# Where q and k are turned: TensorE's transposes replaced by VectorE's 32x32 squares, ScalarE's copies and 96x96 products in a two-layer channel-attention kernel

## The chip, the cores and the metric

The kernel runs on one core of one Trainium2 chip. The metric is the device time of one execution in microseconds (us). Every time below is from executions of this kernel on the chip; durations of single instructions come from one profiled execution.

A core has five engines, each with its own queue of instructions that it works off in order. TensorE (PE in the profile) multiplies matrices into PSUM; each of its multiplications has a weight load ahead of it, which the profile lists apart as PEld. VectorE (DVE), ScalarE (ACT) and GpSimd (POOL) work on SBUF and, the first two, on PSUM. SyncE (SP) issues transfers here. An engine waits for another on semaphores.

## The reference

The input x is an image of 384 channels, 192x192, in fp32. Two layers each add something to x. The first is attention over channels; the second, which the change doesn't touch, a depthwise 7x7 convolution.

```python
# layer 0
qkv = einsum('bchw,oc->bohw', groupnorm(x), w_qkv) + b_qkv         # 384 -> 1152 channels
qkv = qkv.reshape(b, 3*c, 96, 2, 96, 2).max(axis=(3, 5))           # 2x2 max pool
qkv = depthwise_conv3x3(qkv, w_dw) + b_dw                          # 9 taps per channel
q, k, v = split(qkv, 3)                                            # each 8 heads of 48 channels, 9216 places
attn = (q / |q|) @ (k / |k|).T * temperature                       # 48x48 per head, over the 9216 places
out = sum of four top-k softmaxes of attn, each @ v * a_i
x = x + w_proj @ upsample2x(gelu(out)) + b_proj
# layer 1
x = x + depthwise_conv7x7(groupnorm(x), w_sym)
```

The product of q and k sums over the places of the image. TensorE sums over partitions, and the convolutions leave channels on the partitions, so q and k have to be turned: places to the partitions, channels along the free dimension.

## The kernel before

The work runs in stages, one after the other, and the profile's span shows them in this order.

1. **Statistics** (to about 160 us): x is read once for the group norm.
2. **q and k** (about 160 to 1389 us): 24 blocks `b` of 8 image rows (4 pooled rows of 96: 384 places, `PB`). q and k together have 768 channels, 6 tiles `ct` of 128. For each tile, `pooled` (line 639) makes 3 groups `g` of 128x512 in PSUM, each summed over 3 input tiles, and VectorE's `tensor_reduce` (line 647) takes the 2x2 maximum into `ring[ct]`. TensorE runs each fp32 product as two instructions: 54 products, 108 instructions a block. The groups use a pool of 4 PSUM buffers (`pq`), so TensorE can be at most four groups ahead of VectorE's maxima. One tile and one block behind, `depthwise` does the nine taps of block `b-1`: tap 0 is a `tensor_scalar` (line 680), taps 1 to 8 are `scalar_tensor_tensor` (line 682), all on VectorE.
   When six tiles of a block are through, `products` is called (lines 686 to 717): ScalarE squares each tile for the norms (line 691); for each of 3 runs of 128 places and each of two sides, TensorE transposes three 128x128 pieces into a PSUM tile (line 700, 18 instructions a block), ScalarE copies it to SBUF (line 706, 6 copies a block), and 3 products of 128 channels of q with 144 to 192 channels of k are added to `grams` (line 709, 18 instructions a block).
3. **The hand-over** (about 1355 to 1395 us): no further blocks come, VectorE finishes the taps of the last one, TensorE begins the v products on `xv_begun`, and the last products follow.
4. **v** (about 1390 to 2190 us): 16 steps. `convolve` (line 537) makes v; VectorE pools it (line 543) and does its taps (line 905); `attend` (line 961) multiplies v by the attention, in tiles of 128 output channels; `project` (line 985) multiplies by `w_proj`. `attention` itself (lines 772 to 862) is a long chain on VectorE that is worked off between the first v products. It scales `grams` into `scaled`, moves each head's 48x48 part into `att` by DMA, ranks it, and writes `attnT`. Output tile `ct` of 128 channels meets only those input tiles `dt` whose heads overlap it (`near`): 7 pairs of tiles, as 384 channels in heads of 48 don't fall on the bounds of 128.
5. **The 7x7 convolution** (about 2190 us to the end).

The order of instructions on an engine is not always that of the text. A scheduler in the framework reorders them, except where `keep` (`tc.keep_in_program_order`) holds them or `issue_after` sets a lower bound. In the stage for q and k, `keep` isn't used before the change, and the scheduler places the transposes and products of one block among the first groups of the next.

A tile pool with `bufs=n` gives out n buffers in turn; a tile that reuses a buffer waits until all that read the old one are done. Before: `qkp` (the results of the taps) has 9, `trp` (turned sides, squares) 2.

Of the kernel before, what the change touches and what calls it, by code (L numbers as in the profile page):

```python
# [31 lines left out]
NX = 3  # L32
GN_EPS = 1e-5


SPAN = []
for _mt in range(KT):
    _lo = (_mt * P) // HC * HC
    _hi = ((_mt + 1) * P - 1) // HC * HC + HC
    SPAN.append((_lo, _hi))  # L40

PIECES = []
for _mt in range(KT):
# [35 lines left out]
def conv_preact_d2(  # L79
# [146 lines left out]

    ssq = const.tile([P, 2 * KT, NB], F32, name="ssq")
    attnT = const.tile([P, KT, C], F32, name="attnT")


    bctx = ExitStack()
# [26 lines left out]

    psx = ExitStack()
    pgram = psx.enter_context(tc.tile_pool(name="pgram", bufs=1, space=PSUM))  # L260
    gram = []
    for mt, (lo, hi) in enumerate(SPAN):
        o = sum(h - l for l, h in SPAN[:mt])
        gram.append((o, o + hi - lo))
    grams = pgram.tile([P, gram[-1][1]], F32, name="grams")
    gram = [grams[:, lo:hi] for lo, hi in gram]
    ptr = psx.enter_context(tc.tile_pool(name="ptr", bufs=3, space=PSUM))
    qx = ExitStack()
    pq = qx.enter_context(tc.tile_pool(name="pq", bufs=4, space=PSUM))
# [216 lines left out]
        w = wq[:, TWO, i * C : (i + 1) * C]  # L486
        nc.scalar.mul(w, w, rstd0[:, TWO : TWO + 1])
    with tc.issue_after(loaded):
        nc.sync.dma_start(wp, wprojT.rearrange("(t p) o -> p t o", p=P))

# [57 lines left out]

    with ExitStack() as bx:
        padp = bx.enter_context(tc.tile_pool(name="padp", bufs=1))
        qkp = bx.enter_context(tc.tile_pool(name="qkp", bufs=9))
        trp = bx.enter_context(tc.tile_pool(name="trp", bufs=2))

        gwp = bx.enter_context(tc.tile_pool(name="gwp", bufs=1))

# [66 lines left out]
        for ct in range(2 * KT):  # L624
            ring.append(padp.tile([P, 3 * PR + 2, PS + 2], F32, name=f"ring{ct}"))

        def pooled(b, ct, xb):
            rows = xb.rearrange("p t (r c) -> p t r c", c=HW)
            t = ring[ct]
            r0 = 1 + b % 3 * PR  # L630
            for g in range(3):
                begun, there = sums_qk.pop((b, ct, g), (None, False))
                ps = begun
                if not there:
                    ps = pq.tile([P, 512], F32, name=f"pq{b}_{ct}_{g}", tag="pq")
                    if begun is not None:
                        nc.scalar.copy(ps, begun)
                for kt in range(KT) if begun is None else (TWO,):
                    nc.tensor.matmul(  # L639
                        ps,  # L640
                        wq[:, kt, ct * P : (ct + 1) * P],
                        rows[:, kt, :, g * 64 : (g + 1) * 64],
                        start=(kt == 0),
                        stop=(kt == KT - 1),
                        skip_group_check=begun is not None,
                    )
                nc.vector.tensor_reduce(  # L647
                    t[:, r0 : r0 + PR, 1 + g * 32 : 1 + (g + 1) * 32],
                    ps.rearrange("p (h a w b) -> p h w a b", h=PR, a=2, b=2),
                    AX.XY,  # L650
                    ALU.max,
                )
# [22 lines left out]
        def taps(dst, ct, win):  # L675
            for tap in range(9):
                src = win(tap // 3, tap % 3)
                w = wd[:, ct, tap : tap + 1]
                if tap == 0:
                    nc.vector.tensor_scalar(dst, src, w, bdb[:, ct : ct + 1], ALU.mult, ALU.add)  # L680
                else:
                    nc.vector.scalar_tensor_tensor(dst, src, w, dst, ALU.mult, ALU.add)  # L682

# [1 line left out]
            r0 = b % 3 * PR  # L685
            taps(dst, ct, lambda i, j: ring[ct][:, r0 + i : r0 + i + PR, j : j + PS])

        def products(b, qk):
            for i in range(2 * KT):
                junk = trp.tile([P, PB], F32, name=f"junk{b}_{i}", tag="junk")  # L690
                nc.scalar.activation(  # L691
                    junk, qk[i].rearrange("p h w -> p (h w)"), AF.Square,
                    accum_out=ssq[:, i, b : b + 1],
                )
            for j in range(PB // P):
                sides = []
                for s in range(2):
                    ps = ptr.tile([P, C], F32, name=f"tr{b}_{j}_{s}", tag="tr")
                    for i in range(KT):
                        nc.tensor.transpose(  # L700
                            ps[:, i * P : (i + 1) * P],
                            qk[s * KT + i].rearrange("p h w -> p (h w)")[:, j * P : (j + 1) * P],
                            ident,
                        )
                    sb = trp.tile([P, C], F32, name=f"qkT{b}_{j}_{s}", tag=f"qkT{s}")
                    nc.scalar.copy(sb, ps)
                    sides.append(sb)
                for mt, (lo, hi) in enumerate(SPAN):
                    last = nc.tensor.matmul(
                        gram[mt],  # L710
                        sides[0][:, mt * P : (mt + 1) * P],
                        sides[1][:, lo:hi],
                        start=False,
                        stop=(b == NB - 1 and j == PB // P - 1),
                        skip_group_check=True,
                    ).ins
            return last


        nc.tensor.matmul(  # L720
            grams, z[:, RUN : RUN + P], z[:, RUN : RUN + grams.shape[1]], start=True, stop=False,
            skip_group_check=True,
        )
        for b in range(NB + 1):
            xb = None
            if b < NB:
                xb = held.pop(b) if b in held else load_x(b, "xq")
            else:

                qx.close()  # L730
                pv = psx.enter_context(tc.tile_pool(name="pv", bufs=2, space=PSUM))
                xb = xpool.tile([P, 2 * UT, KT, RB * HW], F32, name="xv_begun", tag="xb")
                for kt in range(KT):
                    nc.sync.dma_start(xb[:, :, kt], image_rows(kt, order[0], 0, 2 * UT))
            qk = []
            for ct in range(2 * KT + 1):
                if b < NB and ct < 2 * KT:
                    if b == 0 and ct < 2:

                        if ct == 0:  # L740
                            pooled(b, 0, xb)
                            pooled(b, 1, xb)
                            biases()
                    else:
                        pooled(b, ct, xb)
                    bordered(b, ct)
                if b > 0 and ct > 0:
                    dst = qkp.tile([P, PR, PS], F32, name=f"qk{b}_{ct}", tag="qk")
                    qk.append(dst)
                    depthwise(b - 1, ct - 1, dst)  # L750
                    if ct == 2 * KT:
                        multiplied = products(b - 1, qk)
                    if b == NB:
                        with tc.issue_after(multiplied):
                            for n in ((), (), (0, 1), (), (2, 3), (4,), (5,))[ct]:
                                t0 = n // KT * UT
                                convolve(0, t0, n % KT, xb[:, t0 : t0 + UT], lambda ins: ins)
            if b == 2:
                for tiles in vrows:
                    row_borders(tiles)  # L760
            if b < len(pieces):
                with tc.issue_after(stats0):
                    weights(*pieces[b])

    xctx.close()

    near = {}

    def attention(ap):

# [13 lines left out]
        along_free(rkb, rn[:, KT : 2 * KT], ptr, "rk", "tr")  # L784
        yield

        scaled = ap.tile([P, KT, C // 2], F32, name="scaled")
        for mt, (lo, hi) in enumerate(SPAN):
            nc.vector.scalar_tensor_tensor(
                scaled[:, mt, 0 : hi - lo], gram[mt], rn[:, mt : mt + 1], rkb[:, lo:hi],  # L790
                ALU.mult, ALU.mult,
            )
        att = ap.tile([P, KT, HC], F32, name="att")
        for i, (mt, r0, r1, h) in enumerate(PIECES):
            eng = (nc.gpsimd, nc.scalar)[i % 2]
            o = h * HC - SPAN[mt][0]
            eng.dma_start(att[r0:r1, mt, :], scaled[r0:r1, mt, o : o + HC])
        yield


# [50 lines left out]
            eng.dma_start(diag[r0:r1, mt, h * HC : (h + 1) * HC], mix[r0:r1, mt, :])  # L851
        yield
        for dt in range(KT):
            cts = [ct for ct in range(KT) if SPAN[ct][0] < (dt + 1) * P and SPAN[ct][1] > dt * P]
            near[dt] = cts
            ps = ptr.tile([P, C], F32, name=f"aT{dt}", tag="tr")
            for ct in cts:
                nc.tensor.transpose(
                    ps[:, ct * P : (ct + 1) * P], diag[:, ct, dt * P : (dt + 1) * P], ident
                )  # L860
            lo, hi = cts[0] * P, (cts[-1] + 1) * P
            nc.vector.tensor_copy(attnT[:, dt, lo:hi], ps[:, lo:hi])

# [85 lines left out]
    def attend(i, pin=lambda ins: ins):  # L951
# [2 lines left out]
        gl = gp.tile([P, KT, PBC], F32, name=f"gl{b}", tag="gl")  # L954
        for h in range(2):
            for ct in range(KT):
                dts = [dt for dt in range(KT) if ct in near[dt]]
                ps = ptr.tile([P, C], F32, name=f"po{b}_{ct}_{h}", tag="tr")
                for dt in dts:
                    keep(  # L960
# [563 lines left out]
```

## Time and profile before

| | |
|---|---|
| median of 5 runs | 2798.33 us (2795.73 to 2803.1) |
| the profiled execution | 2799.82 us, span 2798.1 us, granted TensorE clock 0.994 |
| PE busy | 2646.0 us (95%), 8717 instructions |
| DVE busy | 2355.8 us (84%) |
| ACT busy | 873.9 us (31%) |
| POOL busy | 751.0 us (27%) |

Busy is the time in which at least one instruction of the engine was under way. Instructions of one engine overlap at their ends, so the mean duration of one (in ns) is longer than the distance from its start to the next one's; for matmuls by much, as their ends are modelled. In this text, the distance of starts is called the pitch, and work is priced by pitches where the trace shows a row of them. A group's line gives: line of the code, engine, operation, written tile <- read tiles, shapes, count | busy us, mean ns | idle time before it.

### The profile page before, as it was taken

To read this page: it belongs to the slowest core of one execution; us is meant where nothing else is said; L and a number is where in the kernel's file an instruction comes from. 1 tells how busy PE (TensorE), PEld (TensorE's weight loads), DVE (VectorE), ACT (ScalarE), POOL (GpSimd) and SP (SyncE) were. 2 spreads that over 40 slices of the span, in tenths; PEclk is the share of its full clock that TensorE was granted. 3 is DMA by queue.
4 is the path that set the end of the run, shared out by engine and by line. 5 is a ranking of instruction groups with operands and counts; after the bars stand their busy time and mean duration, and the time that the engine had idled before them with its cause. 6 is when DMAs were issued, how large, how long until landed. Compare 5 with 4: busy or idle time off the path is not lost. (4 is left out here: it accounts for less than half of the span.)

```text
span 2798.1 us, 25638 instructions
## 1 busy us (share of the span) xinstructions
PE 2646.0 (95%) x8717; PEld 1586.2 (57%) x8717; DVE 2355.8 (84%) x3383; ACT 873.9 (31%) x1638; POOL 751.0 (27%) x884
## 2 busy tenths in 40 slices
PE   0399999999999999999999999999999899999998
PEld 0144444444445444444556666666666677777776
DVE  7989887887877878878798988889889778888887
ACT  0141111111111111111202232222323577777776
POOL 1024343200000000000102231010101567878876
PEclk9999999999999999999999999999999999999999
DMA  9976656401001001010234998575664899999998
GB/s 380 399 251 208 235 201 220 167 34 68 34 34 68 34 34 68 34 56 13 71 134 170 336 384 312 171 251 194 210 236 153 336 328 357 367 374 373 373 373 262
DMA packets 234002, 580.98 MB, mean 208 GB/s; under 512 B 16608, under 2 KB 165712, under 8 KB 217104
## 3 DMA queue, kind: packets, MB, share of 16 engines
q1 hardware_dynamic: 173376, 283.44, 28.7%
q0 software_dynamic: 37376, 148.85, 15.1%
q10 hardware_dynamic: 23120, 147.07, 14.0%
q8 instruction: 69, 1.13, 0.2%
q14 instruction: 61, 0.50, 0.0%
HBM read 370.93 MB, written 208.21 MB: 207 GB/s over the span
## 5 line engine op out<-in xcount | busy, mean ns | idle before, releaser
L639 PE MATMUL pq<-xq,wq 128*128 128x512 f32 x2268 | 990.7, 592 | 0.0
L639 PEld LDWEIGHTS pq<-xq,wq 128*128 128x128 f32 x2268 | 423.0, 190 | 492.2 <-issue 448.2
L682 DVE SCALAR_TENSOR_TENSOR qk<-ring,wd,qk 128x384 f32<-128x384 f32 x1152 | 675.3, 614 | 20.9 <-ACT ring L669 7.1
L537 PE MATMUL pv<-xv,wq 128*128 128x384 f32 x1656 | 539.2, 486 | 1.4 <-DVE rows L543 1.4
L647 DVE TENSOR_REDUCE ring<-pq 128x128 f32<-128x512 f32 x428 | 294.2, 689 | 192.9 <-PE pq L639 191.2
L1428 PE MATMUL pc<-main,w 128*128 128x288 f32 x1536 | 438.2, 408 | 7.0 <-POOL aux L1356 3.0
L537 PEld LDWEIGHTS pv<-xv,wq 128*128 128x128 f32 x1656 | 314.3, 190 | 217.2 <-DVE rows L543 3.0
L1448 DVE TENSOR_SCALAR apart<-pc,rb 32x576 f32<-32x576 f32 x384 | 312.2, 813 | 80.9 <-PE pc L1428 59.3
L1428 PEld LDWEIGHTS pc<-main,w 128*128 128x128 f32 x1536 | 291.2, 190 | 92.4 <-POOL aux L1356 3.2
L1446 ACT ACTIVATE apart<-pc,rb 32x576 f32<-32x576 f32 x384 | 281.4, 733 | 137.4 <-PE pc L1428 132.6
L905 DVE SCALAR_TENSOR_TENSOR vb<-rows,wd,vb 128x576 f32<-128x576 f32 x384 | 313.2, 817 | 11.2
L1428 PE MATMUL pc<-aux,h 128*128 128x288 f32 x768 | 248.9, 406 | 0.3 <-issue 0.3
L691 ACT ACTIVATE junk<-qk 128x384 f32<-128x384 f32 x144 | 75.4, 524 | 543.5 <-DVE qk L682 543.5
L773 POOL TENSOR_TENSOR rn<-rn,halfpos 128x6 f32<-128x6 f32 x1 | 1.4, 1362 | 850.6 <-DVE rn L772 850.6
L1387 POOL COPY res<-apart 128x1152 f32<-128x1152 f32 (+1 forms) x96 | 224.3, 2363 | 14.0 <-ACT apart L1446 10.2
L1022 DVE TENSOR_TENSOR sx<-xr,y 128x576 f32<-128x576 f32 x180 | 203.9, 1175 | 26.9 <-ACT y L993 21.1
L1063 POOL DMA_DIRECT2D sd<-sx x96 | 72.4, 757 | 488.7 <-DVE sx L1022 469.8
L543 DVE TENSOR_REDUCE rows<-pv 128x192 f32<-128x768 f32 x144 | 137.7, 956 | 53.5 <-PE pv L537 53.3
L1271 DVE SCALAR_TENSOR_TENSOR w<-eye,sb,w 128x512 f32<-128x512 f32 x96 | 174.0, 1851 | 1.5
L1428 PEld LDWEIGHTS pc<-aux,h 128*128 128x128 f32 x768 | 145.4, 189 | 41.9 <-POOL main L1336 0.8
L1042 ACT ACTIVATE wq<-sx,negmid 128x1152 f32<-128x1152 f32 x96 | 120.7, 1257 | 94.2 <-DVE sx L1022 90.1
L985 PE MATMUL pr<-gl,wp 128*128 128x288 f32 x576 | 142.6, 406 | 0.0
(226 smaller groups left out, 2108.5 us busy)
## 6 DMA issues: line engine op xcount, KB each, us to landing
sd<-sx POOLq DMA_DIRECT2D x96, 600.0 KB, 9.8
out_dram<-res SPq DMA_DIRECT2D x192, 288.0 KB, 11.1
main<-sd ACTq DMA_DIRECT2D x46, 1200.0 KB, 5.2
xv<-in_x_dram SPq DMA_DIRECT2D x138, 384.0 KB, 6.4
xr<-in_x_dram SPq DMA_DIRECT2D x45, 1152.0 KB, 11.7
xq<-in_x_dram SPq DMA_DIRECT2D x21, 2304.0 KB, 8.0
w<-wt ACTq DMA_DIRECT2D x46, 1024.0 KB, 7.1
xs<-in_x_dram SPq DMA_DIRECT2D x24, 1536.0 KB, 15.2
```

Of the source, the lines that this page charges most:

```text
L537: nc.tensor.matmul(ps[:, u, 0 : RB * HW], wq[:, kt, o : o + P], xb[:, u, kt, :], start=(kt == 0), stop=(kt == KT - 1),)
L639: nc.tensor.matmul(ps, wq[:, kt, ct * P : (ct + 1) * P], rows[:, kt, :, g * 64 : (g + 1) * 64], start=(kt == 0), stop=(kt == KT - 1), skip ...
L647: nc.vector.tensor_reduce(t[:, r0 : r0 + PR, 1 + g * 32 : 1 + (g + 1) * 32], ps.rearrange("p (h a w b) -> p h w a b", h=PR, a=2, b=2), AX. ...
L682: nc.vector.scalar_tensor_tensor(dst, src, w, dst, ALU.mult, ALU.add)
L905: pin(nc.vector.scalar_tensor_tensor(dst, src, w, dst, ALU.mult, ALU.add))
L985: nc.tensor.matmul(ps[:, 0:H], wp[:, ct, ot * P : (ot + 1) * P], gl[:, ct, h * H : (h + 1) * H], start=(ct == 0), stop=(ct == KT - 1),)
L1022: nc.vector.tensor_tensor(bass.AP(flat.tensor, flat.offset + at(e) + a * RUN, [flat.ap[0], [JP, NT], [1, NJ], [at(f) - at(e), 2]],), xq[:, ...
L1271: nc.vector.scalar_tensor_tensor(mid, eye.unsqueeze(1).to_broadcast([P, 4, P]), sb[:, c : c + 1], mid, ALU.mult, ALU.add,)
L1387: keep(copy(res[ps, k], apart[ps, :, k].rearrange("p e n -> p n e")))
L1428: nc.tensor.matmul(ahead[q][:, k, 0 : NT * NJ], lhs, rhs, start=(j == 0), stop=(j == 2), skip_group_check=True,)
L1446: keep(nc.scalar.mul(dst, src, scale))
L1448: keep(nc.vector.tensor_scalar_mul(dst, src, scale))
```

## The change

- **q and k.** Tap 0 of the nine goes from VectorE to ScalarE. Behind a tile's last tap, VectorE transposes all 32x32 squares of the 128x384 tile in one instruction, into `turns`. That turns each square in itself but leaves the squares where they were; ScalarE then copies 32 partitions of `turns` (3 x 3 x 32 elements) at a time to the partitions where they belong, 16 copies a side, 32 a block. The squares for the norms are written to a PSUM tile.
- **The products.** They are no longer 128 channels of q by 144 or 192 of k, but two heads at a time: 96 of q by 96 of k, 4 for each of the 3 runs of places, 12 a block (24 instructions). They are done one iteration later (`products(b - 2, done)`) and are pinned: one after each product of the convolution, from tile 3 of the block on, and at the hand-over between the products on `xv_begun`. `qkp` now has 5 buffers, `trp` 1.
- **attention.** `grams` now holds 96 partitions by 384 columns. One multiplication scales it along k, the DMAs go to `att` from there, and q's factor is multiplied on `att` after the DMAs.
- **v.** The output channels of the attention are turned by 96 (`TURN`): tile 0 holds channels 96 to 223, and so on. A tile then meets two input tiles, not two or three (`MEET`): 6 pairs in place of 7. `wprojT` is loaded in that order, in three DMAs. `attnT` is cleared once on POOL.

The core of the diff:

```diff
+PAIR = 2 * HC
+TURN = PAIR
+MEET = [[dt for dt in range(KT) if any(
+            (TURN + ct * P + j) % C // HC in range(dt * P // HC, ((dt + 1) * P - 1) // HC + 1)
+            for j in range(P))] for ct in range(KT)]
...
-        qkp = bx.enter_context(tc.tile_pool(name="qkp", bufs=9))
-        trp = bx.enter_context(tc.tile_pool(name="trp", bufs=2))
+        qkp = bx.enter_context(tc.tile_pool(name="qkp", bufs=5))
+        trp = bx.enter_context(tc.tile_pool(name="trp", bufs=1))
...
+        between = []
+        def pinned(ins):
+            if ins.ins.engine != mybir.EngineType.PE:
+                return ins
+            keep(ins)
+            while between and next(between[0], between) is between:
+                between.pop(0)
+            return ins
...
+                    if b > 1:
+                        pinned(ins)
...
-                    nc.vector.tensor_scalar(dst, src, w, bdb[:, ct : ct + 1], ALU.mult, ALU.add)
+                    nc.scalar.activation(dst, src, AF.Identity, bias=bdb[:, ct : ct + 1], scale=w)
...
+        Q = 32
+        def squares(b, ct, t):
+            junk = ptr.tile([P, C], F32, name=f"junk{b}_{ct}", tag="tr")
+            nc.scalar.activation(junk, t, AF.Square, accum_out=ssq[:, ct, b : b + 1])
+        def turned(side, turns):
+            for a in range(P // Q):
+                for f in range(P // Q):
+                    nc.scalar.copy(
+                        side[f * Q : (f + 1) * Q].rearrange("p c (t n) -> p t c n", n=P)[
+                            :, :, :, a * Q : (a + 1) * Q],
+                        turns[a * Q : (a + 1) * Q].rearrange("p t (c n) -> p t c n", n=P)[
+                            :, :, :, f * Q : (f + 1) * Q])
+                yield
+        def products(b, sides):
+            nonlocal multiplied
             for j in range(PB // P):
+                for lo in range(0, C, PAIR):
+                    multiplied = keep(nc.tensor.matmul(
+                        grams[0:PAIR, lo : lo + PAIR],
+                        sides[0][:, j, lo : lo + PAIR], sides[1][:, j, lo : lo + PAIR],
+                        start=False, stop=(b == NB - 1 and j == PB // P - 1),
+                        skip_group_check=True)).ins
+                    yield
...
+            done, sides = sides, []
             for ct in range(2 * KT + 1):
+                if ct == (KT if b < NB else 1) and done:
+                    between.append(products(b - 2, done))
...
+                    nc.vector.transpose(turns[:, t], flat)
+                    squares(b - 1, ct - 1, flat)
+                    for _ in copies:
+                        pass
+                    if t == KT - 1:
+                        side = trp.tile([P, PB // P, C], F32, name=f"qkT{b}_{s}", tag=f"qkT{s}")
+                        sides.append(side)
+                        copies = turned(side, turns)
+                        for _ in range(2):
+                            next(copies)
...
+        nc.vector.tensor_tensor(scaled[0:PAIR], grams[0:PAIR], rkb[0:PAIR], ALU.mult)
...
+        nc.vector.tensor_tensor(
+            att, att, rn[:, 0:KT].unsqueeze(2).to_broadcast([P, KT, HC]), ALU.mult)
...
-                dts = [dt for dt in range(KT) if ct in near[dt]]
+                dts = MEET[ct]
```

## The prediction

> **What bounds it now.** I first read the engines' busy time by windows (columns: PE, PEld, DVE, ACT, POOL, clock, DMA share, GB/s). A block lasts 51 us, so the first row is one block of the stage for q and k; the second lies in the stage for v.
>
> ```profile
> core 0: us, PE busy (x) PEld busy (x) DVE busy (x) ACT busy (x) POOL busy (x), PEclk, DMA share, GB/s
> 741.00:792.00 51.00, 50.98 (x145) 24.69 (x144) 40.97 (x72) 7.94 (x24) 0.00 (x0) 1.00 0.12 47
> 1730.00:1780.00 50.00, 50.00 (x172) 32.49 (x171) 44.72 (x51) 13.67 (x30) 4.15 (x7) 1.00 0.64 213
> ```
>
> TensorE has no idle time in either; VectorE has 10 us of 51 free, ScalarE 43. So what TensorE sheds here shortens the run until VectorE is late. Next, what it does between two blocks, from its timeline (start, length, x count):
>
> ```profile
> 699.45 42.65 PE L639 MATMUL pq<-xq,wq 128*128 128x512 f32 x99
> 741.94 1.50 PE L700 MATMUL tr<-ident,qk 128*128 128x128 f32 x10
> 743.27 1.02 PE L639 MATMUL pq<-xq,wq 128*128 128x512 f32 x2
> 744.13 0.49 PE L700 MATMUL tr<-ident,qk 128*128 128x128 f32 x3
> 744.46 1.02 PE L639 MATMUL pq<-xq,wq 128*128 128x512 f32 x2
> 745.32 0.38 PE L700 MATMUL tr<-ident,qk 128*128 128x128 f32 x2
> 745.54 1.02 PE L639 MATMUL pq<-xq,wq 128*128 128x512 f32 x2
> 746.40 1.79 PE L709 MATMUL grams<-qkT,qkT 128*128 128x144 f32 x12
> 748.03 0.49 PE L700 MATMUL tr<-ident,qk 128*128 128x128 f32 x3
> 748.36 1.02 PE L639 MATMUL pq<-xq,wq 128*128 128x512 f32 x2
> 749.22 1.01 PE L709 MATMUL grams<-qkT,qkT 128*128 128x144 f32 x6
> 750.07 20.33 PE L639 MATMUL pq<-xq,wq 128*128 128x512 f32 x47
> ```
>
> Read starts, not lengths, which overlap. 99 convolution instructions take 42.49 us: a pitch of 0.429. From 741.94 to 750.07 are 8.13 us, of which 8 convolution instructions are 3.43. The 18 transposes and 18 products thus cost **4.70 us a block**; the groups' busy time (68.2 + 91.6 us over 24 blocks, 6.7 each) would overstate it. 108 x 0.429 + 4.70 = 51.0, the block's length. In the v stage:
>
> ```profile
> 1566.09 23.38 PE L537 MATMUL pv<-xv,wq 128*128 128x384 f32 x72
> 1589.31 6.95 PE L961 MATMUL po<-vb,attnT 128*128 128x288 f32 x28
> 1596.10 11.77 PE L537 MATMUL pv<-xv,wq 128*128 128x384 f32 x36
> ```
>
> 28 attention products take 6.79 us: 0.2425 each. Pitches for 512, 384 and 288 columns (0.429, 0.3225, 0.2425) lie on a line of 0.83 ns a column; 96 columns give 0.083.
>
> **Part by part.** All sums are against the profiled execution, 2799.8 us.
>
> *Products between convolutions.* Per block 4.70 us go and 12 products (24 instructions) come. The first instruction's weights load behind a convolution; the second's load can hide only behind 0.083 us, and so can those of the next convolution. What a load costs when little hides it, this row shows (24 in 2.68 us, to the next start):
>
> ```profile
> 166.89 2.82 PE L470 MATMUL bias_ps<-mean,wq 128*128 128x1 f32 x24
> 169.57 5.38 PE L639 MATMUL pq_begun<-xs,wq 128*128 128x512 f32 x8
> ```
>
> 0.112 for 128 columns of weights. No row has 96; between three quarters of that and the whole, a pair costs 0.084 to 0.112 plus 0.112, so 0.196 to 0.224; pure streaming would be 0.166. I take 0.20: 2.4 us a block, **2.3 us saved**. Blocks of the convolution that hold such products: iterations 2 to 23, 22 of them: **-50.6** (ends -44 and -60).
>
> *VectorE.* It loses six first taps a block (mean 502 ns, median 475) and gains six transposes of 128x384. No row shows a transpose. The nearest is that `tensor_scalar` of the same shape, one read and one write: 0.475. Below lies the 128x128 `tensor_scalar` (0.28), above line 1271's two-input form, 1.85 for 128x512, so 1.39 for 384. At 0.475 VectorE stays at 41.0 us in a block of 48.7; at 1.39 it is at 46.5, still under. So nothing for this, and 7.7 us of cover; past about 1.75 us each it would set the pace.
>
> The Trainium skill ("VectorE: DVE Perf Modes", The three transpose paths) gives VectorE 311 ns for 128x128 bf16 squares, to TensorE's 390. Three times that, 933 ns, is an estimate for 128x384; by it VectorE stands at 43.8 us and the sum is the same.
>
> *ScalarE.* Per block 6 copies go; 6 first taps (the square of the same shape: 0.52) and 32 copies of 32x288 elements come. Copies of 128x96, 32x256 and 32x512 take 0.27, 0.40 and 0.62: 0.43 here; as ends overlap (two of line 706 take 0.86, not 2 x 0.479), the pitch is 0.33 to 0.43, and I take 0.38. The dear end is line 1387 on ScalarE, strided, 2.17 for 1152, so about 0.68. Its block: 3.2 + 4.3 (squares) + 12 to 22 + 1 = 21 to 30 us of 48.7. Not a bound by amount. By order: a burst of 16 copies stands in its queue (6.1 us, dear end 10.9), and the next first taps behind it. In the changed program's instruction order the burst for q stands behind the product that frees its buffer (tile 4's first group); VectorE has the tap behind it three groups, 8.1 us, later. Covered at 6.1 + 0.5; at the dear end VectorE is 3.3 us late, which its free 7.7 us and the four buffers of `pq` (three groups of lead, 7.7 us) hide. Nothing, then. The second burst ends some five groups before TensorE's products want it.
>
> *The start.* In the first two blocks, ScalarE also fills PSUM and 27 borders (about 9 us), and in the new order a tap stands behind them. Zero to 5; I take **+1.5**.
>
> *The hand-over.* Here the change adds a wait. In the new order TensorE runs one `pv` product after the last convolution and then the first pinned product, which needs the second burst of block 22. Count from R, where TensorE leaves the convolution (1355.55 before). VectorE still has a maximum, seven taps (pitch 0.53) and a transpose: R+5.2. ScalarE: two squares (0.62) and 16 copies (0.38): R+12.5. So TensorE stands for some 12 us, with all v products queued behind. Then 72 `pv` at 0.3225 less the pair done, 22.6; twelve pairs, 2.4; the last twelve, back to back at 0.1, 2.4; factors (lines 779 and 224), 1.5: R+41.4. The last block's taps, its copies and VectorE's three waiting maxima end by R+36, inside that. Before, the first `pv<-xv` started at 1393.01, R+37.5. So **+3.9**; the 4.7 x 2 that TensorE sheds here are lost in the wait. `attention` begins 3.4 later against the v products. TensorE got to its `aT` at 1476.2; the DMAs that `aT` needs had been issued at 1465.6 to 1468.7, so about 5 us of cover; **+1**. The new multiplication on `att` waits for DMAs that the first ranking waited for anyway.
>
> *v.* Each step loses 4 of 28 instructions: 0.97 us. In 13 steps TensorE is the bound, VectorE has 5 of 50 us free: **-12.6**. The last three attends wait for VectorE and ScalarE in part: **-1**. Two more DMAs on SP (its issues take 0.37 each), one cleared tile on POOL (1.07) at the start, an extra copy to `attnT`: beside idle queues, nothing; uncovered, some 2 us.
>
> Sum: -50.6 + 1.5 + 3.9 + 1 - 12.6 - 1 = **-57.8**: 2742.0 for the profiled execution. That one was 1.5 above the median of the runs, so **2740** against the median of 2798.3. With its ends: 2727 to 2757.
>
> **Rivals.**
>
> *VectorE waits for ScalarE.* The chain convolution, maximum, first tap, taps, transpose, copies, product now passes through ScalarE twice, with `qkp` cut to 5 and `trp` to 1. If copies are at the dear end and waits on both bursts don't find the free time, half of the saving in the blocks goes: about 2767, and 2757 to 2785. For it: busy shares hide order, and the instruction order has groups without taps where VectorE can only stand. Against: 7.7 us free a block.
>
> *The narrow product drains TensorE* (slower). Every product now lies between two of other width. A convolution's modelled length is 0.592 at a pitch of 0.429; if each change of width lets the array run empty, it costs that difference, 0.163, twice a pair: 24 x 0.163 = 3.9 us a block, 90 us in all: 2830. It decides from 0.41 us a pair (57.8 us over 276 pairs above my 0.20). Against: the six instructions of line 779, of 8 rows, start 0.127 apart amid 128-row ones and show no such gap. For: no row has fewer weight columns.
>
> Here the Trainium skill speaks against the change: "TensorEngine Tiling (Array Packing)", Key Properties, says that changing the tiling mode drains TensorE. Its modes have 128, 64 or 32 columns; it doesn't say what 96 count as. By the one reading the sum stays, by the other it is the rival's.
>
> *A transpose over 1.75 us or a copy over 1.2 us.* VectorE or ScalarE becomes the bound, and the gain is eaten: 2790 to 2805. No row is so dear for so little.
>
> **The numbers.** Forecast 0.62 (2727 to 2757), better than that 0.07, VectorE late 0.17, drains 0.09, dear transposes or copies 0.05. The range 2722 to 2780 leaves out the slow cases, the end of the late one and the best. Faster by over 0.2% (about what a measurement of this kernel can tell from no change) 0.87, within 0.03, slower 0.10.
>
> **What would show it.** Right: a block of 48.7 us with TensorE without idle time, pairs adding 0.2, VectorE near 41 us a block; 24 `po` a step and 49 us a step; some 12 us of idle TensorE at the hand-over, released by ScalarE's copies. Wrong: TensorE's loads of `pq` waiting for VectorE's maxima, VectorE waiting for ScalarE's first taps (rival one); gaps at each pair (rival two); a transpose above 1.4 us.

## The result, and the profile after

The changed kernel takes 2797.52 us (median of 30 runs) where the kernel before takes 2797.46 (50 runs): a ratio of 0.9999, 95% interval 0.9993 to 1.0004. The forecast was 2740. The profiled execution took 2801.11 us (span 2799.3). The time didn't stay the same because nothing happened: TensorE's work fell as forecast, and the blocks kept their length.

First the same two stretches as before (columns as in the prediction):

```profile
741.00:792.00 51.00, 48.52 (x131) 22.01 (x130) 37.99 (x68) 23.06 (x56) 0.00 (x0) 1.00 0.14 54
1730.00:1780.00 50.00, 50.00 (x171) 32.30 (x170) 45.59 (x53) 14.07 (x32) 4.49 (x6) 1.00 0.66 219
```

In the blocks TensorE now has 2.5 us of 51 idle. The starts of the first product of each block (252.09 at first, 1325.96 at last, 21 blocks) give 51.14 us a block; before, by the first transpose of each, it was 51.15. ScalarE went from 8 to 23 us. VectorE has no more work than before (41.2 us, mean of four windows), and yet TensorE waits for it. The waits say for what VectorE waits (engine, line waited for: us, times, longest). Before the change, what VectorE waited for most in this stage was TensorE, for its maxima:

```profile
DVE ring L647 <- PE pq L639: 191.2, 133, 1.9
```

After:

```profile
DVE qk L710 <- ACT qk L706: 162.4, 73, 6.0
...
PEld pq L663 <- DVE ring L673: 94.4, 117, 2.8
...
DVE qk L710 <- ACT ring L695: 38.4, 14, 5.4
PE pq L663 <- DVE ring L673: 37.9, 29, 1.9
ACT qk L706 <- DVE turns L793: 24.2, 47, 1.3
```

Now its taps (line 710) wait 201 us for ScalarE: for the first taps (706) and the small copies of border rows (695). Over 22 blocks that is 9.1 a block, and 41.2 + 9.1 is the block but for 0.8. Read the last line too: where the first tap (line 706) itself waits, it waits for a **transpose**, not for the maxima that it reads. One such wait on VectorE's timeline, and ScalarE beside it:

```profile
777.72 0.58 DVE L793 STREAM_TRANSPOSE turns<-qk 128x384 f32<-128x384 f32 x1
778.23 1.85 DVE L673 TENSOR_REDUCE ring<-pq 128x128 f32<-128x512 f32 x3
786.03 2.21 DVE L710 SCALAR_TENSOR_TENSOR qk<-ring,wd,qk 128x384 f32<-128x384 f32 x4 [5.95 <-ACT qk L706]
```

```profile
778.25 7.02 ACT L727 COPY qkT<-turns 32x288 f32<-32x288 f32 x16
785.29 0.71 ACT L706 ACTIVATE qk<-ring,bdb,wd 128x384 f32<-128x384 f32 x1
```

With the transpose at 777.72, and the square for the norms that ScalarE does beside it, a tile is done, its buffer is free, and the next first tap could start. But in ScalarE's queue the 16 copies of a side stand ahead of it. VectorE does three maxima that were waiting (1.85 us); the next instruction in its queue is a tap on the tile that the first tap begins. For 5.95 us it does nothing, with the later maxima behind it. TensorE runs through its four buffers of `pq` and stops as well:

```profile
753.73 6.28 PE L663 MATMUL pq<-xq,wq 128*128 128x512 f32 x14 [0.85 <-DVE ring L673]
759.85 0.33 PE L743 MATMUL grams<-qkT,qkT 128*96 128x96 f32 x2
760.01 1.05 PE L663 MATMUL pq<-xq,wq 128*128 128x512 f32 x2
760.90 0.33 PE L743 MATMUL grams<-qkT,qkT 128*96 128x96 f32 x2
...
788.89 11.43 PE L663 MATMUL pq<-xq,wq 128*128 128x512 f32 x26 [1.64 <-DVE ring L673]
```

Between two waits the new products are as cheap as forecast: one returns each 1.055 us, where two convolution instructions take 0.858, so a pair costs 0.197. In the v stage a step is

```profile
1598.94 5.98 PE L1017 MATMUL po<-vb,attnT 128*128 128x288 f32 x24
...
1648.32 1.86 PE L1017 MATMUL po<-vb,attnT 128*128 128x288 f32 x7
```

49.38 us from start to start, 50.35 before. Against the profile before: TensorE leaves the q and k convolutions at 1350.64 (1355.55 before), begins `pv<-xv` at 1398.86 (1393.01), gets to `aT` at 1487.57 (1476.23), and ends 645.6 us after that with the v products (655.3).

### The profile page after: what moved, and what is told of

The parts are those of the page before. It is cut to its first block, busy times and chain, and to the rows that moved or that the text cites. A ratio compares the mean times of both kernels' runs of the same rounds, so it can differ in the third digit from the quotient of the medians.

```text
span 2799.3 us, 25696 instructions
## 1 busy us (share of the span) xinstructions
PE 2592.3 (93%) x8365; PEld 1522.2 (54%) x8365; DVE 2327.4 (83%) x3383; ACT 1234.1 (44%) x2406; POOL 753.5 (27%) x885
## 3 DMA queue, kind: packets, MB, share of 16 engines
q10 hardware_dynamic: 23120, 147.07, 14.1%
## 4 chain that ended last, share of the span: by engine, by line
PE 44%; issue 34%; DMA 12%; POOL 6%; DVE 4%; ACT 0%; SPq 0%; ACTq 0%; POOLq 0%; DVEq 0%
PE pc L1484 19%; PE pv L549 18%; DMA wt<-g 5%; PE pr L1041 4%; PE po L1017 3%; DMA wh<-g 3%; DMA xs<-in_x_dram 2%; POOL wt L593 2%; POOL g L578 2%; POOL g L582 1%; DVE sx L1078 1%; DVE st L323 1%; DVE vb L961 1%; DMA xv<-in_x_dram 1%; DMA bp<-in_bproj_dram 1%
## 5 line engine op out<-in xcount | busy, mean ns | idle before, releaser
L663 PE MATMUL pq<-xq,wq 128*128 128x512 f32 x2268 | 1035.0, 599 | 37.9 <-DVE ring L673 37.9
L663 PEld LDWEIGHTS pq<-xq,wq 128*128 128x128 f32 x2268 | 408.7, 191 | 475.9 <-issue 369.6
L727 ACT COPY qkT<-turns 32x288 f32<-32x288 f32 x768 | 328.9, 428 | 28.7 <-DVE turns L793 10.0
L673 DVE TENSOR_REDUCE ring<-pq 128x128 f32<-128x512 f32 x428 | 287.3, 680 | 3.9 <-PE pq L663 3.5
L1443 POOL COPY res<-apart 128x1152 f32<-128x1152 f32 (+1 forms) x96 | 217.7, 2298 | 50.9 <-DMA out_dram<-res 47.6
L743 PEld LDWEIGHTS grams<-qkT,qkT 128*96 128x96 f32 x576 | 92.7, 164 | 147.0 <-issue 135.7
```

The source lines that it names most:

```text
L663: ins = nc.tensor.matmul(ps, wq[:, kt, ct * P : (ct + 1) * P], rows[:, kt, :, g * 64 : (g + 1) * 64], start=(kt == 0), stop=(kt == KT - 1) ...
L673: nc.vector.tensor_reduce(t[:, r0 : r0 + PR, 1 + g * 32 : 1 + (g + 1) * 32], ps.rearrange("p (h a w b) -> p h w a b", h=PR, a=2, b=2), AX. ...
L727: nc.scalar.copy(side[f * Q : (f + 1) * Q].rearrange("p c (t n) -> p t c n", n=P)[:, :, :, a * Q : (a + 1) * Q], turns[a * Q : (a + 1) * Q ...
L1443: keep(copy(res[ps, k], apart[ps, :, k].rearrange("p e n -> p n e")))
```

## The experiments

Three theories for the 51.1 us block. **T1**: the bursts of 16 copies stand in ScalarE's queue ahead of what VectorE needs next. **T2**: the first taps lack buffers (`qkp`, 9 cut to 5). **T3**: VectorE's own work has become the bound.

All runs at a glance; a block is the mean distance of first products. Each ratio is to the kernel before on the same chip, with its 95% interval.

| run | edit to the changed kernel | ratio | block, us |
|---|---|---|---|
| (the change) | | 0.9999 [0.9993, 1.0004] | 51.14 |
| e1_tap_on_vector | tap 0 on VectorE | 0.9881 [0.9866, 0.9897] | 49.27 |
| e2_four_copies | 4 copies a side, not 16; squares stay on their partitions | 0.9795 [0.9781, 0.9809] | 48.71 |
| e3_nine_buffers | 9 buffers | 0.9817 [0.9803, 0.9832] | 48.71 |
| e4_v_alone | (the kernel before, with the v part alone) | 0.9980 [0.9966, 0.9993] | 51.16 |
| f1_nine_late_pins | 9 buffers, later pins | 0.9806 [0.9792, 0.9819] | 48.71 |
| f2_six_buffers | 6 buffers | 0.9990 [0.9981, 0.9999] | 51.06 |
| f3_nine_tap_on_vector | 9 buffers, tap 0 on VectorE | 0.9817 [0.9804, 0.9831] | 48.71 |
| f4_four_buffers | 4 buffers | 1.0002 [0.9993, 1.0011] | 51.14 |
| g1_seven_buffers | 7 buffers | 0.9793 [0.9774, 0.9811] | 48.71 |
| g2_products_at_once | 9 buffers, products at once | 0.9776 [0.9759, 0.9793] | 48.71 |
| g3_nine_without_v | 9 buffers, v part undone | 0.9829 [0.9811, 0.9848] | 48.71 |
| g4_double_copies | 9 buffers, each copy twice | 1.0390 [1.0367, 1.0412] | 54.98 |

The four e runs were on a chip on which the kernel before takes 2821.55 us; the others on chips where it takes 2797 to 2799. So ratios are compared, and times only within a group.

### Bursts, buffers or VectorE's work: e1, e2, e3

```diff
 # e1
-nc.scalar.activation(dst, src, AF.Identity, bias=bdb[:, ct : ct + 1], scale=w)
+nc.vector.tensor_scalar(dst, src, w, bdb[:, ct : ct + 1], ALU.mult, ALU.add)
 # e2
-for f in range(P // Q): nc.scalar.copy(side[f*Q:(f+1)*Q]..., turns[a*Q:(a+1)*Q]...)
+nc.scalar.copy(side...[:, :, :, a*Q:(a+1)*Q], turns...[:, :, :, a*Q:(a+1)*Q])
 # e3
-qkp = bx.enter_context(tc.tile_pool(name="qkp", bufs=5))
+qkp = bx.enter_context(tc.tile_pool(name="qkp", bufs=9))
```

> Tap 0 of q and k goes back to VectorE; the transposes, ScalarE's copies and the pinned products stay. Three theories for the block of 51.1 us. T1 (ScalarE's bursts of 16 copies, 7.0 us, stand ahead of the next first tap in its queue, and VectorE, with 41.2 us of work a block, waits about 9 us for them): the taps no longer go through ScalarE, VectorE has six taps of about 0.49 more (44.1 us a block) and the blocks come near TensorE's 48.8, at most 49.5 with what the halo copies still hold; 2755 to 2770 us. T2 (the taps on ScalarE wait for one of only five buffers): the same gain, so this run does not tell T1 from T2. T3 (VectorE's own work with the transposes has become the bound): 2.9 us more work for it a block, so 2800 to 2860.

> The placing of the squares is left out: each side is copied by 4 copies over all 128 partitions, without moving a square to other partitions, so the output is not the reference's. First taps stay on ScalarE, with five buffers. A burst is 4 copies of some 0.44 us, 1.75 us in place of 7.0. T1 (the bursts): VectorE's waits for ScalarE, 201 us in the changed kernel, shrink to a third or less, the block comes to TensorE's 48.8; 2750 to 2765 us. T2 (first taps short of buffers): no gain, 2790 to 2801. T3 (VectorE's work): no gain, 2790 to 2801.

> The results of the taps have 9 buffers again, as before the change; nothing else. T2 (a first tap on ScalarE waits until one of five buffers is free): its waits go and most of the gain comes back, 2750 to 2770 us. T1 (the bursts of copies stand ahead of the tap): the taps may be issued further ahead of a burst, so a part, 2775 to 2800. T3 (VectorE's work): nothing, 2795 to 2803.

Measured: 2785.67, 2761.50 and 2768.62 us. T3 falls: with six taps more, VectorE is busy for 47.2 us in windows of 51 (41.2 in the changed kernel), and the blocks are shorter, not longer. But e2 and e3 both bring the whole 48.71, which neither T1 nor T2 alone had foretold: T2 gave short bursts no gain, T1 gave buffers a part. So neither is the cause by itself; it takes long bursts **and** few buffers. In e1, mostly, two blocks of three are 48.71 and the third about 50.4, where the border copies, still on ScalarE, stand behind a burst (32.1 us of waits).

### How many buffers: f2, f4, f3

My next theory was one of amount: each buffer puts a first tap one tile further ahead of the burst.

```diff
-qkp = ... bufs=5        # f2: bufs=6    f4: bufs=4    f3: bufs=9, tap 0 on VectorE as in e1
```

> Six buffers for the results of the taps in place of five; nothing else. Theory: a first tap waits until the tile five before has been turned, and a burst of 16 copies (7.0 us) then stands ahead of it in ScalarE's queue. One more buffer puts each tap one tile earlier in the queue, 8 us ahead, which is more than a burst: nearly all comes back, a block of 48.7 to 49.5 us in place of 51.1, a ratio to the kernel before of 0.980 to 0.988. Rival (only the sum of the waits counts, so each buffer brings about a quarter of what four bring): a block of about 50.5, a ratio of 0.994 to 0.997.

> Four buffers in place of five; nothing else. Theory: each first tap is queued one tile later still, behind the same bursts, and VectorE has one tile less to work on meanwhile: its waits for ScalarE, 201 us with five, grow by the time of some 4 to 8 us a block, so a block of 55 to 59 us and a ratio to the kernel before of 1.03 to 1.07. Rival (the buffers are not what the taps wait for): 0.99 to 1.01.

> Nine buffers, and tap 0 back on VectorE. With five buffers and the tap on VectorE two blocks of three were 48.71 us, as with nine buffers and the tap on ScalarE, and the third 50.4: there the small copies of border rows stand behind a burst. Theory (what costs is work that VectorE waits for, queued behind a burst): with nine buffers VectorE has other tiles' taps to do meanwhile, its 44 us a block are below 48.7, so all blocks at 48.7 and the same time as nine buffers with the tap on ScalarE within 5 us, a ratio of 0.981 to 0.984. Rival (VectorE needs the 2.9 us a block that ScalarE takes from it): 0.986 to 0.992.

Measured: 2795.87, 2798.11 and 2746.78 us. The theory of amount falls on both sides: four, five and six buffers give the same blocks (within 0.1 us) and the same waits. Of four buffers, from 250 to 1330 us (five in the same stretch 160.6, six 157.5):

```profile
DVE qk L710 <- ACT qk L706: 160.3, 71, 6.0
```

f3 agrees with its first theory: with nine buffers VectorE can keep tap 0, the blocks are 48.71, and the ratio is that of e3 (on another chip).

What four, five and six share is seen in the order of ScalarE's instructions. A run of it around the burst for q, for five buffers (the block of the timelines above) and for seven (as in most blocks), with the border copies left out and the tiles found by counting (tap 706, square 721, copies 727; the number behind `qk_` is the tile, old the block that is being closed, new the next):

```
five                                   seven
721 square qk_3 (old)                  706 tap qk_4 (new)
706 tap    qk_2 (new)                  721 square qk_4 (old)
721 square qk_4 (old)                  727 copies x16
727 copies x16                         706 tap qk_5 (new)
706 tap    qk_3 (new)                  721 square qk_5 (old)
721 square qk_5 (old)                  706 tap qk_6 (new)
706 tap    qk_4 (new)
```

Taps 6 to 8 of a tile need a row that comes with the next block's maxima, six tiles later. The same maxima let the first tap of the next block's tile begin. So by its data a tile is opened before the one six back is closed: **seven tiles are open at once**. With fewer buffers the first tap cannot follow its data; it waits until a tile is closed (its last three taps, its transpose and its square done), and a burst that has its place there comes in between. With four and with six buffers the row is that of five, with the first tap of the tile before (`qk_2`) or behind (`qk_4`) in the place of `qk_3`: another tile is opened there, by the same closing and behind the same burst.

The changed kernel's trace holds a comparison of its own. In 12 of its blocks the burst for q stands ahead of the tap on `qk_3`, as in the list; there VectorE waits 5.3 to 6.0 us for that tap. In 8 blocks the tap stands ahead of the burst; there no wait at this burst is longer than 1.1 us. At the burst for k VectorE waits 3.1 to 5.4 us in every block but the first.

So I expected a threshold:

### The threshold, and the bursts once more: g1, g4

```diff
 # g1
-qkp = ... bufs=5
+qkp = ... bufs=7
 # g4: bufs=9, and
+for _ in range(2):
     nc.scalar.copy(side[...], turns[...])
```

> Seven buffers for the results of the taps. Four, five and six gave the same time, so it is no matter of amount. Theory: taps 6 to 8 of a tile need the maxima of the next block, six tiles later, and the same maxima let the first tap of the tile six further on start. So seven tiles are open at once by the data. With six buffers or fewer the first tap waits for a buffer in place of its data: it can only follow the transpose of an older tile, and where that is the third of a side, the burst of 16 copies as well. With seven it depends on the maxima again: as with nine, blocks of 48.71 us, a ratio to the kernel before of 0.980 to 0.984. Rival (there is no such threshold, and what helps is memory placed elsewhere or eight and more buffers): 0.995 to 1.001.

> Nine buffers, and each of the 32 copies of a block done twice, so that a burst is 14.1 us in place of 7.0; ScalarE's work grows from about 23 to 37 us of a block, still no bound by amount. Theory (nine buffers put first taps about one tile, 8.1 us, ahead of a burst; the coupling through ScalarE's queue is still there): a burst longer than 8.1 us makes VectorE wait again, 5 to 6 us for each of two bursts, against 5 us a block that VectorE has free: blocks of 51 to 56 us, 2800 to 2880 us where the kernel before takes 2798, a ratio of 1.00 to 1.03. Rival (the buffers alone were the cause, and the length of a burst does not count once they are enough): blocks of 48.71, 0.980 to 0.984.

Seven buffers: 2740.69 us, all blocks 48.71. The waits of the same name as above:

```profile
ACT qk L706 <- DVE ring L673: 139.2, 34, 5.5
...
DVE ring L673 <- PE pq L663: 50.6, 61, 1.4
...
DVE qk L710 <- ACT ring L695: 41.7, 40, 2.7
DVE qk L710 <- ACT qk L706: 40.7, 27, 2.1
```

The first tap waits for its maxima (139.2), no longer for a transpose; VectorE's wait for it is a quarter, and VectorE's maxima wait for TensorE again. With the comparison of the blocks above, this settles the cause: the threshold lies between six and seven, as counted from the code.

Bursts doubled, with nine buffers: 2906.56 us, and VectorE waits again:

```profile
DVE qk L710 <- ACT qk L706: 230.0, 35, 8.2
...
DVE qk L710 <- ACT ring L695: 65.4, 28, 4.1
```

So buffers don't dissolve the coupling through ScalarE's queue; they give a lead, and a burst of 14.1 us is longer than it. The direction is as foretold, the size more (blocks 52.7, 55.6 and 58.0 in turn, a ratio of 1.039 for 1.00 to 1.03): the border copies wait behind bursts as well, which I had not counted.

### The v part: e4, g3

```diff
 # e4: the kernel before, with TURN, MEET, wprojT in three DMAs and attnT cleared
 # g3: bufs=9, and these undone
-dts = MEET[ct]
+dts = [dt for dt in range(KT) if ct in near[dt]]
```

> The kernel before with the last part of the change alone: the attention's output channels turned by 96, 24 products a step in place of 28, wprojT in three DMAs, attnT cleared once. The prediction priced this at -12.6 us for 13 steps and -1 for the last attends; from the changed kernel's trace the stage for v is 9.7 us shorter. If the parts add up, 2786 to 2790 us; if the shorter steps are lost to VectorE or the transfers, 2795 to 2799.

> Nine buffers, and the part for v undone: the attention's channels as before the change, 28 products a step in place of 24. What is left is the part for q and k. The steps were 50.35 us before and 49.38 after, so 13 steps and the last attends are 11 to 13 us, less some 3 that the transfers take back: 8 to 11 us more than nine buffers with it, a ratio to the kernel before of 0.985 to 0.986. Rival (the v part brings nothing by the end of the run): 0.981 to 0.983.

e4: 2814.03 us, by the ratio 5.6 less than before (interval 2 to 10), where 10 to 13 were forecast. In its trace the steps are 49.38 us, but one is 75.8: TensorE waits 22.6 us for a transfer of `xv`, and e3 on the same chip 22.3. If the transfer alone sets the end of that wait, what the steps ahead of it save is lost there; no trace of the kernel before on this chip shows it. g3: 2751.64 us. Its ratio, 0.9829, lies in the range of its rival (the part brings nothing), and by e3's 0.9817 the rival would hold; but e3 was on the chip with the long wait. On g3's own chip g1 takes 10.95 us less, and differs by the v part and by two buffers that g1's blocks don't need. So where that wait is short (the step with it is 2.2 us longer in g3, 0.5 in g1) the part brings about 11.

### The hand-over: f1, g2

With seven buffers TensorE still stands 2.85 and 7.93 us at the hand-over.

```diff
 # f1 (bufs=9)
-if ct == (KT if b < NB else 1) and done:
+if ct == (KT if b < NB else 4) and done:
 # g2: the same, and
+    if b == NB:
+        for _ in between.pop(): pass
```

> Nine buffers for the results of the taps, and at the hand-over the pinned products begin two v products' tiles later (24 v instructions stand ahead of the first, 7.7 us). With nine buffers alone TensorE stood 2.87 and 8.08 us there and then ran some 4 us at half its pitch. If the order of the pins makes that wait, the 8.1 us go and the slow stretch with them: 8 to 11 us less than with nine buffers alone, so a ratio to the kernel before of about 0.978 to 0.979 (0.9817 with nine buffers). If VectorE's backlog is what ends last at the hand-over, the wait only moves to the v products, whose two PSUM buffers wait for VectorE: 0 to 3 us.

> Nine buffers, and at the hand-over the products of block 22 come at once behind the first 24 v products, in place of one after each v product. With nine buffers alone TensorE waits 8.1 us for the copies of block 22; with its first pins behind 24 v products it no longer does, but the 32 copies of block 23 (14.1 us) wait until the twelve spread products (9.8 us) have freed the sides, and TensorE waits 4.2 us for those. Back to back the twelve pairs take 2.2 us, so the copies start 7 us sooner and lie beside 48 v products (15.5 us): 5 to 8 us less than nine buffers alone, a ratio to the kernel before of about 0.979 (0.9817 with nine buffers, 0.9806 with later pins). Rival (the attention's own chain on VectorE decides when the stage goes on): 0.981 to 0.982.

f1: 2742.94 us, 0.9806, against e3's 0.9817 no more than its rival allowed (nine buffers alone weren't run on f1's chip). The wait moved: 32 copies (14.09 us) now wait for the spread products to free the sides, and TensorE waits 4.2 us for the copies. g2 lets them go at once:

```profile
1303.04 8.01 PE L549 MATMUL pv<-xv_begun,wq 128*128 128x384 f32 x24 [2.84 <-DVE ring L673]
1312.54 0.41 PE L743 MATMUL grams<-qkT,qkT 128*96 128x96 f32 x2 [1.49 <-ACT qkT L727]
1314.31 3.48 PE L743 MATMUL grams<-qkT,qkT 128*96 128x96 f32 x22 [1.36 <-ACT qkT L727]
1317.58 16.00 PE L549 MATMUL pv<-xv_begun,wq 128*128 128x384 f32 x48
1333.41 2.20 PE L743 MATMUL grams<-qkT,qkT 128*96 128x96 f32 x24
```

2736.55 us, 0.9776: `aT` starts 6.5 us earlier than with seven buffers (1424.75 for 1431.24). This is the best version, 2.2% under the kernel before; against seven buffers (0.9793) the intervals overlap.

## Why the prediction was wrong

- **Products between convolutions**: right. Pairs 0.197 (0.20), blocks of 48.71 (48.7) wherever VectorE isn't late. With seven buffers TensorE leaves the convolutions 56.6 us earlier than before: 53.7 in 22 blocks (before they were 51.15, every third being 51.3 to 51.6, and I had taken 51.0), and 2.9 elsewhere, for +1.5 at the start: a wait of TensorE for ScalarE there (1.9 us) is gone.
- **The narrow product drains TensorE**: refuted by the 0.197.
- **VectorE**: right. The transpose takes 0.572 us (0.475 taken, ends 0.28 and 1.39), its work 41.2 us a block (41.0).
- **ScalarE**: here it failed. The sizes were off, the copy's within its dear end of 0.68: a copy has a pitch of 0.439 (0.38), a first tap takes 0.704 (0.52; I took the square's row, which has no scale or bias per partition), a burst 7.0 us (6.1). But the step that broke is "VectorE has the tap behind it three groups, 8.1 us, later", and with it "Nothing, then". I read places in the instruction order as times at TensorE's pace. VectorE had three maxima waiting, did them in 1.85 us, and stood at the tap. And I quoted "`qkp` cut to 5" only in a rival, as if buffers were an amount; counting the open tiles (seven) would have shown that every first tap now hangs on the closing of an older tile, with a burst between the two once or twice a block.
- **The rival "VectorE waits for ScalarE"** was the right one, at 0.17 and at half its price: it let half of the saving in the blocks go, and all went. Nor was its condition met, copies at the dear end: copies of 0.439 were enough. Its free 7.7 us a block were to take the lateness up; the waits came to 9.1, and each also stopped the maxima behind it.
- **The hand-over**: with seven buffers +5.8 (43.3 us from R to `pv<-xv`, before 37.5) for +3.9; the two waits are 10.8 us for "some 12". Not priced: TensorE then runs at half its clock (below). In the change itself +10.8, as VectorE came to the hand-over late (TensorE waits 6.70 for its maxima).
- **attention**: +5.5 in the change, +5.7 with seven buffers, for +1. TensorE waits 3.5 and 0.7 us for VectorE's maxima of v, 1.4 before. The rest is the clock again (below): with seven buffers it is 0.50 from 1357.5, behind the longer wait, to 1363.5, and the 96 products from 1357.54 take 34.19 us, 3 more than at a pitch of 0.3225; before, it is 1.00 throughout this part.
- **v**: the step right to the hundredth (0.97); about 11 by g3 for 12.6 and 1. In the change one step is 2.7 us longer, where TensorE waits for `xv`.

With seven buffers the sum is 59.3 us by spans (2798.1 to 2738.8), for 57.8. The forecast describes that kernel, not this one, and fits even that one in part by luck: blocks and start gave 7.5 us more than forecast, the hand-over and attention took 6.6 more.

Two rules of the Trainium skill bear on the failed step. "Perfetto Trace Analysis", Optimization Strategy, says that the same gap repeating on the engine that should be saturated can mean that there is no room for the next tile, and names the number of buffers: so it is here, with TensorE idle for 2.5 us of 51, though it waits for VectorE, and VectorE's releaser is named as ScalarE, no buffer. "ScalarE: Activation LUTs", What ACT_TABLE_LOAD costs, gives 186 ns, 0.833 ns an element and 93 ns for each per-partition operand; an estimate by it is 692 ns for the first tap and 426 for a copy, where this trace has 704 and 428.

## What to carry to other kernels

Where a change cuts a pool's buffers, count how many tiles the data keep open at once, from the first write of one to the last read of the oldest; below that number each new tile hangs on the closing of an old one, and all that is queued between the two is on the path. A free share of an engine covers nothing for an instruction that stands first in its queue: ask what is *next* in the queue when the awaited one is late. And a burst of small instructions is harmless only as long as it is shorter than the lead of what is queued behind it.

## What the runs showed of the hardware

**Behind long waits TensorE came back at half its clock, though not behind each.** At the hand-over of the kernel with seven buffers, by windows (the clock is the third number from the end), and the rows of TensorE:

```profile
1294.00:1302.00 8.00, 5.15 (x13) 1.93 (x12) 7.93 (x16) 1.38 (x4) 0.00 (x0) 1.00 0.00 0
1303.00:1311.00 8.00, 0.56 (x1) 0.00 (x0) 7.79 (x14) 5.74 (x15) 0.00 (x0) 0.50 0.00 0
1311.00:1316.00 5.00, 4.51 (x12) 2.73 (x13) 2.20 (x6) 4.86 (x15) 0.00 (x0) 0.52 0.55 194
1316.00:1324.00 8.00, 8.00 (x39) 5.24 (x38) 3.04 (x8) 0.66 (x2) 1.36 (x1) 1.00 0.90 322
```

```profile
1301.99 1.57 PE L549 MATMUL pv<-xv_begun,wq 128*128 128x384 f32 x2 [2.85 <-DVE ring L673]
1311.49 0.64 PE L743 MATMUL grams<-qkT,qkT 128*96 128x96 f32 x2 [7.93 <-ACT qkT L727]
...
1313.26 0.64 PE L743 MATMUL grams<-qkT,qkT 128*96 128x96 f32 x2
...
1315.02 0.53 PE L743 MATMUL grams<-qkT,qkT 128*96 128x96 f32 x2
...
1316.22 0.33 PE L743 MATMUL grams<-qkT,qkT 128*96 128x96 f32 x2
```

Behind the wait of 2.85 us the v product already takes 1.57 us, where later ones take 0.84. After 7.93 us more of waiting a pair and its v product take 1.77 us, twice, then 1.20, and then 0.84: some 2.2 us lost behind the wait. In the block from 741 to 792 us of the changed kernel the waits of 0.9 to 1.6 us leave the clock at 1.00. Its longest in the blocks, five of 1.93 us, differ: behind two of them (552.6 and 1016.8) the clock is 0.50 for 3.4 us, behind the others it stays. Nor does the length alone decide among longer ones: the wait of 2.84 us in g2 at the place of the 2.85 above leaves the clock at 1.00, and so does one of 3.50 us in g4 (at 947.1).

**These copies of 32 partitions don't overlap.** 16 copies of 32x288 take 7.02 us, 0.439 each, longer than one (0.428). The four copies over 128 partitions in e2 also last 0.428, but follow each other by 0.33:

```profile
751.66 1.42 ACT L726 COPY qkT<-turns 128x288 f32<-128x288 f32 x4
```

My 0.38 came from the overlap of copies over all partitions. The copies of 32 also move between partitions; which of the two makes the difference wasn't separated.
